# A decoder layer on one core: the first batch's weights, chunks and scales in another order

## The chip, the core and the metric

The kernel runs on one core of a Trainium2 chip. Five engines work side by side, each in the order of its own instructions: TensorE (PE, matmuls and transposes; its weight loads are listed apart as PEld), VectorE (DVE), ScalarE (ACT), GpSimd (POOL) and SyncE (SP), which here only issues DMAs. They wait for each other through semaphores. The metric is the device time of one execution in microseconds (us), the median of several runs.

## The reference, cut to what matters

The layer has three parts, each with a layer norm ahead and a residual behind: self attention, cross attention and a feed-forward block. x is 8 batches of 256 rows of 1024. The change touches the start of the self attention alone:

```python
def bitnet_linear(x, weight, scale_param):
    s = jnp.maximum(jnp.mean(jnp.abs(weight), axis=1), 1e-08)
    binary_w = jnp.sign(weight / s[:, None])
    y = jnp.einsum('bsi,oi->bso', x, binary_w)
    y = y * (s * scale_param)[None, None, :]
    return jnp.nan_to_num(y, nan=0.0, posinf=1000000.0, neginf=-1000000.0)
...
q, k, v = three bitnet_linear of layernorm(x)    # 32 heads for q, 8 for k and v, 32 wide
scores = jnp.einsum('bhqd,bhkd->bhqk', q, k) / np.sqrt(HEAD_DIM)
attn = jax.nn.softmax(scores, axis=-1)
out = jnp.einsum('bhqk,bhkd->bhqd', attn, v)
return bitnet_linear(out, o_weight, o_scale)
```

So every weight row gives a scale (the mean of its absolute values) and a row of signs. q, k and v need signs to multiply with, and scales to multiply the product with.

## The kernel before, in words

**Weights.** The four weight matrices are cut into 20 blocks of 128 rows by 1024: two of k, eight of q, two of v, eight of o. `blocks` lists them in the order in which they are loaded; the place in this list is the block's number. Before, 0 and 1 are k, 2 and 3 are q's first two, 4 and 5 are v, 6 to 11 the rest of q, 12 to 19 o. For a block, `weight_load` (lines 276 to 296) issues its DMAs on SP: one of 512 KB for k and v, four of 128 KB for q, eight of 64 KB for o. `weight_turn` turns it by 8 PE transposes into two PSUM banks, and ACT writes the signs from there (Sign, L313). `weight_sum` takes the sum of absolute values on DVE (L302), then a small operation on DVE (s, L304) and three on POOL (L305 to L307), which leave the scale in `scol`. Eight blocks have room at once; the list `after` says which block is loaded into the room of which, when that has been turned and summed. SP issues in order, so a load that waits for its room holds up those behind it.

**Projections.** x of a batch, normed and turned, is kept as a high and a low part (`xh`, `xl`), so that a chunk of 128 columns of q or k takes 16 matmuls. In the first batch, `first_chunk` (L425 the matmuls, L431 to L440 what follows) makes a chunk alone: ACT scales it (y), and five operations of DVE, six for k, make it finite and scale it. Later chunks come in pairs as parts (`q_parts`, L403, L412): there `nan_to_num` spreads the work over DVE and POOL, and its last operation, a copy_predicated on DVE (L361), is put off until two parts later (`later`, `settle`). v scales columns, not rows, so that its scales, and o's, have to lie along the free dimension: `scale_part` makes diagonal tiles of `scol` on POOL (dg, L331) ahead of time, multiplies them with ones on PE (L338), and DVE copies the result to `v_sc` or `o_sc` (L339).

**Order.** Everything is issued in an order that is written out by hand. A prologue loads, norms x of batch 0, turns blocks 0 to 3 and makes both k chunks and two q chunks. Then `step` runs 8 times for each batch, once for every four heads (c, from 0 to 7); below, step c is that of the first batch. A step issues the scores of its four heads (L549), DVE's row maxima (nm, L692), the turning of the previous step's probabilities (L528, copied by ACT, L532), then the parts that `self_plan` lists for this step, with the exponentials of ACT (L711) and the divisions by the sums (`over_sums`: on DVE, POOL or ACT, as the table `BY` says with a letter for each head) between them, and last the product with v (L587). Steps 0 to 3 use k chunk 0, steps 4 to 7 k chunk 1.

The parts of the first batch's steps before:

```python
[weight(4), weight(5), v0[0], weight(6), weight(7)]
+ [scale_part(10, 2, v_sc), v0[1]],
mixed(q_parts(st, 2) + q_parts(st, 4), [weight(8), weight(9), weight(10)]),
[weight(11)] + q_parts(st, 6) + [weight(12)],
[weight(13)] + ln[:2] + [weight(14)] + ln[2:],
k[:1] + [weight(15)] + k[1:],
...
```

Here `weight(i)` is turn, sum and the next load, `ln` are the four parts that norm and turn x of batch 1 (xn, L155; the turns at L163; xh, L348; xl, L349), and `k`, `v` are projections of batch 1.

**PSUM.** All these parts take their PSUM tiles from `bank`, in a fixed turn over three banks; a tile waits until the one three places before it (or two of three, by the pool) has been read. The scores have four banks of their own.

Of the kernel before, what the change touches and what calls it, by code (L numbers as in the profile page):

```python
# [13 lines left out]
AF = mybir.ActivationFunctionType  # L14
# [21 lines left out]
def decoder_layer(  # L36
# [214 lines left out]
    def block(put, t, col, w, q=False, o=False):  # L251
        a = State()
        a.put, a.t, a.col, a.rows, a.q, a.o = put, t, col, w, q, o
        blocks.append(a)

    def columns(dst, t):
        return lambda e0: dst[:, e0 : e0 + 4, t * P : (t + 1) * P]

    for t in range(2):
        block(columns(kT_w, t), t, 8 + t, kw)  # L260
    for c in range(2):
        block(columns(qT_w[c], 0), c, c, qw, q=True)
    for t in range(2):
        block(columns(vT_w, t), t, 10 + t, vw)
    for c in range(2, EC):
        block(columns(qT_w[c], 0), c, c, qw, q=True)
    for t in range(EC):
        block(columns(oT_w, t), t, 12 + t, ow, o=True)

# [9 lines left out]
    def weight_load(i):  # L279
        a = blocks[i]  # L280
        a.w = wk_.tile([P, E], F32, tag=where[i], name="w")
        if a.q:
            gh, r = a.t // 4, a.t % 4
            for j in range(4):
                r0 = ((gh * 4 + j) * 4 + r) * HD
                nc.sync.dma_start(a.w[j * HD : (j + 1) * HD, :], a.rows[r0 : r0 + HD, :])
        elif a.o:

            rows = a.rows[a.t * P : (a.t + 1) * P, :]
            for c in range(EC):  # L290
                nc.sync.dma_start(
                    a.w[:, c * P : (c + 1) * P].rearrange("p (j d) -> p j d", d=HD),
                    rows.rearrange("p (g j r d) -> p g r j d", g=2, j=4, r=4)[:, c // 4, c % 4],
                )
        else:
            nc.sync.dma_start(a.w, a.rows[a.t * P : (a.t + 1) * P, :])

    def weight_sum(i):

        a = blocks[i]  # L300
        total = small.tile([P, 1], F32, tag="rs", name="total")
        nc.vector.tensor_reduce(total, a.w, AX.X, ALU.add, apply_absolute_value=True)  # L302
        s = small.tile([P, 1], F32, tag="s", name="s")
        nc.vector.tensor_scalar(s, total, 1.0 / E, 1e-8, ALU.mult, ALU.max)  # L304
        nc.gpsimd.tensor_scalar_mul(total, total, 0.0)  # L305
        nc.gpsimd.tensor_add(s, s, total)
        nc.gpsimd.tensor_mul(scol[:, a.col : a.col + 1], s, pcol[:, a.col : a.col + 1])  # L307

    def weight_turn(i):

        a = blocks[i]
        for h in range(2):
            nc.scalar.activation(  # L313
                a.put(4 * h), four_T(a.w[:, h * 512 : (h + 1) * 512], "ps_w"), AF.Sign
            )

    def weight_next(i):

        weight_turn(i)
        weight_sum(i)  # L320
        for k in after.get(i, []):
            weight_load(k)

    def scale_part(col0, n, dst, soon=False):

        box = {}

        def ahead():
            box["dg"] = wk_.tile([P, n, P], F32, tag="xn", name="dg", bufs=2)
            for k in range(n):  # L330
                nc.gpsimd.tensor_scalar_mul(  # L331
                    box["dg"][:, k, :], ident, scol[:, col0 + k : col0 + k + 1]
                )

        def main():
            ps = bank([P, n, P], "ps_d")
            for k in range(n):
                nc.tensor.matmul(ps[:, k, :], ones, box["dg"][:, k, :], start=True, stop=True)  # L338
            nc.vector.tensor_copy(dst, ps.rearrange("p k c -> p (k c)"))  # L339

        return Part(0.3 * n, main, ahead, soon)

    def weight(i):
        return Part(1.1, lambda: weight_next(i))


    def split(hi, lo, src):
# [19 lines left out]
    def ln_parts(st, b):  # L367


        def ahead(q):  # L370
            t, h = q // 2, q % 2
            need(st)
            st.xn = getattr(st, "xn", {})
            st.xn[q] = normed_half(xb[b][t], st.mv[:, t, 0:1], st.rs[:, t : t + 1], h)

        def main(q):
            t, h = q // 2, q % 2
            if q == 0:
                st.xh = wk_.tile([P, EC, S], F32R, tag="xh", name="xh")
                st.xl = wk_.tile([P, EC, S], F32R, tag="xl", name="xl")  # L380
            ps = four_T(st.xn.pop(q), "ps_t")
            e4, t4 = slice(h * 4, (h + 1) * 4), slice(t * P, (t + 1) * P)
            split(st.xh[:, e4, t4], st.xl[:, e4, t4], ps)

        return [Part(0.5, lambda q=q: main(q), lambda q=q: ahead(q), True) for q in range(2 * TB)]
# [56 lines left out]
    def q_parts(st, c0):  # L442
        return proj_T(
            st, lambda i, e: qT_w[c0 + i][:, e, :], c0, lambda: st.qT[:, c0 : c0 + 2, :]
        )
# [3 lines left out]
    def k_parts(st):  # L449
        def dst():  # L450
            st.kT = wk_.tile([P, 2, S], F32, tag="kT", name="kT", bufs=2)
            st.qT = wk_.tile([P, EC, S], F32, tag="qT", name="qT", bufs=2)
            return st.kT

        def then():
            nc.vector.tensor_scalar_mul(st.kT, st.kT, K_SCALE)

        return proj_T(st, lambda i, e: kT_w[:, e, i * P : (i + 1) * P], 8, dst, then)
# [645 lines left out]
    def tail(fb, j):  # L1104
# [14 lines left out]


    BY = {
        0: ["DDDD", "PPPD", "PPPD", "PPPP", "PPPD", "PPPD", "DDDD", "PPPD"],
        1: ["DDAA", "PPAA", "PPAA", "DDDA", "DDAA", "DDDA", "DDDA", "DDDA"],
        B - 1: ["DDAA", "DDDA", "DDAA", "PPAA", "PPAA", "DDDA", "DDDA", "DDDA"],
    }
# [8 lines left out]
    def mixed(a, b):  # L1134
        out = []
        for i in range(max(len(a), len(b))):
            out += a[i : i + 1] + b[i : i + 1]
        return out
# [4 lines left out]
    def self_plan(b):  # L1143
        st = sts[b]
        if b == 0:
            nxt = sts[1]
            v0 = v_parts(st)
            ln, k, v = ln_parts(nxt, 1), k_parts(nxt), v_parts(nxt)
            return [
                [weight(4), weight(5), v0[0], weight(6), weight(7)]  # L1150
                + [scale_part(10, 2, v_sc), v0[1]],
                mixed(q_parts(st, 2) + q_parts(st, 4), [weight(8), weight(9), weight(10)]),
                [weight(11)] + q_parts(st, 6) + [weight(12)],
                [weight(13)] + ln[:2] + [weight(14)] + ln[2:],
                k[:1] + [weight(15)] + k[1:],
                mixed(v, [weight(16), weight(17)]),
                mixed(q_parts(nxt, 0), [weight(18), scale_part(12, 4, o_sc[:, 0:512], True)])
                + [weight(19)],
                mixed(q_parts(nxt, 2), [scale_part(16, 4, o_sc[:, 512:1024])]),
            ]  # L1160
        o = o_all(sts[b - 1])
        if b + 1 < B:
            nxt = sts[b + 1]
            ln = ln_parts(nxt, b + 1)
            return [
                q_parts(st, 4) + q_parts(st, 6),
                o[0][:1] + ln[:2] + o[0][1:],
                o[1][:1] + ln[2:] + o[1][1:],
                k_parts(nxt),
                o[2] + v_parts(nxt),  # L1170
                o[3],
                q_parts(nxt, 0),
                q_parts(nxt, 2),
            ]
        x0 = xts[0]
        ln = lnx_parts(x0)
        return [
            q_parts(st, 4) + q_parts(st, 6),
            o[0],
            o[1],  # L1180
            o[2][:1] + ln[:2] + o[2][1:],
            o[3][:1] + ln[2:] + o[3][1:],
            ctx_parts(x0, (act, dve)) + ckv_part(x0),
            cq_part(x0) + ckvT_part(x0),
            cqk_parts(x0, (dve, act)),
        ]
# [62 lines left out]
    with tc.manual_schedule(  # L1249
# [12 lines left out]
        ln_moments(st, 0)  # L1262
        need(st)
        weight_turn(0)
        st.xh = wk_.tile([P, EC, S], F32R, tag="xh", name="xh")
        st.xl = wk_.tile([P, EC, S], F32R, tag="xl", name="xl")
        lo = []
# [13 lines left out]
        for a in lo:  # L1281
            nc.vector.tensor_sub(*a)
        weight_turn(1)
        for i in range(2):
            weight_sum(i)
        for i in range(2):
            for k in after.get(i, []):
                weight_load(k)
        st.kT = wk_.tile([P, 2, S], F32, tag="kT", name="kT", bufs=2)
        st.qT = wk_.tile([P, EC, S], F32, tag="qT", name="qT", bufs=2)  # L1290
        for i in range(2):
            first_chunk(
                st, lambda e: kT_w[:, e, i * P : (i + 1) * P], 8 + i, st.kT[:, i, :], K_SCALE
            )
            weight_next(2 + i)
        for i in range(2):
            first_chunk(st, lambda e: qT_w[i][:, e, :], i, st.qT[:, i, :])
        xb[1] = load_x(1)

        prev = None  # L1300
# [94 lines left out]
```

## Time and profile before

| | |
|---|---|
| time, median of 3 runs | 1546.89 us (1545.93 to 1547.07) |
| the profiled execution, its own time | 1546.57 us |
| its span in the profile | 1544.8 us |
| PE busy | 1511.1 us, 98% of the span |
| DVE, ACT, POOL busy | 62%, 52%, 26% |
| mean granted clock of TensorE | 0.995 |
| PE busy, 0 to 70 us and 70 to 130 us | 54.2 and 52.7 us |
| PE busy, 130 to 1545 us | 1404.2 us |

A line of the timeline gives start and length in us, engine, line of the kernel, operation, output and inputs, shape and number of instructions, and in brackets how long the engine sat idle before it and what ended that. A row of the table of stretches gives the stretch and its length, the busy time and number of instructions of PE, PEld, DVE, ACT and POOL, the clock granted to TensorE (1.00 is full speed), the share of the DMA engines and what they moved.

### The profile page before, as it was taken

To read this page: it belongs to the slowest core of one execution; us is meant where nothing else is said; L and a number is where in the kernel's file an instruction comes from. 1 tells how busy PE (TensorE), PEld (TensorE's weight loads), DVE (VectorE), ACT (ScalarE), POOL (GpSimd) and SP (SyncE) were. 2 spreads that over 40 slices of the span, in tenths; PEclk is the share of its full clock that TensorE was granted. 3 is DMA by queue.
4 is the path that set the end of the run, shared out by engine and by line. 5 is a ranking of instruction groups with operands and counts; after the bars stand their busy time and mean duration, and the time that the engine had idled before them with its cause. 6 is when DMAs were issued, how large, how long until landed. Compare 5 with 4: busy or idle time off the path is not lost.

```text
span 1544.8 us, 25713 instructions
## 1 busy us (share of the span) xinstructions
PE 1511.1 (98%) x9494; PEld 1015.2 (66%) x9494; DVE 956.7 (62%) x1878; ACT 799.2 (52%) x2450; POOL 402.8 (26%) x475
## 2 busy tenths in 40 slices
PE   6899999999999999999999999999999999999998
PEld 5777888888888887777777777544444444444443
DVE  7878898999989899766676665343233233323322
ACT  4677898989898888755566666311111111111110
POOL 2555453545354534022221211131001100100000
PEclk9989999999999999999999999999999999999999
DMA  9430020101020141212444311110011002000001
GB/s 234 68 83 18 26 69 29 56 29 65 19 69 28 60 153 45 85 42 71 152 152 168 107 63 77 62 41 0 0 56 54 0 7 102 1 0 27 28 0 54
DMA packets 67917, 92.78 MB, mean 60 GB/s; under 512 B 40475, under 2 KB 46417, under 8 KB 67665
## 3 DMA queue, kind: packets, MB, share of 16 engines
q1 hardware_dynamic: 63184, 74.37, 15.6%
q0 software_dynamic: 4608, 16.78, 2.7%
q8 instruction: 75, 1.23, 0.3%
q14 instruction: 50, 0.40, 0.1%
HBM read 65.44 MB, written 25.17 MB: 59 GB/s over the span
## 4 chain that ended last, share of the span: by engine, by line
PE 88%; DVE 5%; ACT 3%; DMA 2%; POOL 1%; issue 1%; SPq 0%; DVEq 0%; ACTq 0%; POOLq 0%
PE ps_h L1045 19%; PE ps_pt L528 10%; PE ps_z L1089 9%; PE ps_q L403 8%; PE ps_o L496 7%; PE s L549 4%; PE po L587 4%; PE ps_p L1019 4%; PE ps_o L1108 4%; PE s L625 3%; PE po L648 3%; PE ps_q L855 2%; PE ps_qk L870 2%; PE ps_t L163 2%; PE ps_o L665 2%; PE ps_v L470 2%
## 5 line engine op out<-in xcount | busy, mean ns | idle before, releaser
L711 ACT ACTIVATE p<-s,nm 128x256 f32<-128x256 f32 x768 | 359.7, 520 | 0.4 <-DVE nm L692 0.4
L532 ACT COPY pT<-ps_pt 128x512 f32<-128x512 f32 x384 | 197.3, 599 | 170.1 <-PE ps_pt L528 169.6
L1057 ACT ACTIVATE sg<-ps_h,b_col 128x512 f32<-128x512 f32 (+1 forms) x88 | 59.6, 678 | 413.5 <-PE ps_h L1045 413.5
L692 DVE TENSOR_REDUCE nm<-s 128x2 f32<-128x512 f32 x384 | 237.5, 678 | 9.2 <-PE s L625 6.0
L1058 DVE SCALAR_TENSOR_TENSOR sg<-ps_h,b_col,sg 128x512 f32<-128x512 f32 (+1 forms) x88 | 65.0, 739 | 273.1 <-ACT sg L1057 273.1
L528 PE MATMUL ps_pt<-ident,p 128*128 128x128 f32 x1536 | 194.6, 279 | 1.8 <-DVE o_sc L339 1.0
L711 ACT ACTIVATION_READ_ACCUMULATOR p<-s,nm 128x1 f32 x768 | 193.4, 252 | 0.0
L528 PEld LDWEIGHTS ps_pt<-ident,p 128*128 128x128 f32 x1536 | 164.3, 141 | 41.5 <-issue 26.6
L1089 PE MATMUL ps_z<-ac,u_sb 128*128 128x512 f32 x336 | 157.7, 593 | 0.0
L403 PE MATMUL ps_q<-xh,qT_w 128*128 128x256 f32 x496 | 121.7, 287 | 0.0
L403 PE MATMUL ps_q<-xl,qT_w 128*128 128x256 f32 x496 | 118.9, 281 | 0.0
L1345 POOL TENSOR_TENSOR x2t<-x2t,b_sb 128x1024 f32<-128x1024 f32 x16 | 37.6, 2357 | 296.2 <-DVE xn L155 296.2
L680 POOL TENSOR_TENSOR x1t<-x1t,y 128x256 f32<-128x256 f32 x64 | 47.3, 759 | 232.7 <-DVE y L673 230.2
L1089 PEld LDWEIGHTS ps_z<-ac,u_sb 128*128 128x128 f32 x336 | 61.9, 190 | 68.8 <-issue 68.8
L356 POOL TENSOR_SCALAR tmp<-y 128x512 f32<-128x512 f32 x78 | 58.4, 749 | 182.1 <-DVE y L505 103.1
L496 PE MATMUL ps_o<-oT_w,oh 128*128 128x512 f32 x256 | 105.9, 414 | 0.0
L496 PE MATMUL ps_o<-oT_w,ol 128*128 128x512 f32 x256 | 101.0, 395 | 0.0
L403 PEld LDWEIGHTS ps_q<-xh,qT_w 128*128 128x128 f32 x496 | 93.3, 188 | 1.6
L403 PEld LDWEIGHTS ps_q<-xl,qT_w 128*128 128x128 f32 x496 | 93.4, 188 | 0.0
L572 DVE TENSOR_SCALAR p<-p,sm 128x256 f32<-128x256 f32 x250 | 87.4, 406 | 7.9
L1045 PE MATMUL ps_h<-pT,w_ffn 128*128 128x512 f32 (+1 forms) x184 | 88.7, 577 | 0.0
L1045 PE MATMUL ps_h<-late,w_ffn 128*128 128x512 f32 (+1 forms) x184 | 88.7, 577 | 0.0
(159 smaller groups left out, 2731.7 us busy)
## 6 DMA issues: line engine op xcount, KB each, us to landing
xs<-in_x_dram SPq DMA_DIRECT2D x32, 512.0 KB, 4.2
x<-xs POOLq DMA_DIRECT2D x16, 512.0 KB, 3.0
x1t<-x SPq DMA_DIRECT2D x16, 512.0 KB, 6.0
c<-in_ctx_dram SPq DMA_DIRECT2D x16, 512.0 KB, 3.9
x<-x1t POOLq DMA_DIRECT2D x16, 512.0 KB, 3.8
x2t<-x SPq DMA_DIRECT2D x16, 512.0 KB, 5.0
out_dram<-x2t SPq DMA_DIRECT2D x32, 256.0 KB, 2.0
w<-in_L_attn_q_weight_dram SPq DMA_DIRECT2D x32, 128.0 KB, 5.8
```

Source lines behind the costliest of these rows:

```text
L403: nc.tensor.matmul(ps[:, i, :], w(i, e), x_[:, e, :], start=(e == 0 and x_ is st.xh), stop=(e == EC - 1 and x_ is st.xl),)
L496: nc.tensor.matmul(ps, o_[c // 4][:, c % 4, t * P : (t + 1) * P], oT_w[:, c, h * 512 : (h + 1) * 512], start=(c == 0 and o_ is st.oh), sto ...
L528: nc.tensor.transpose(ps[:, k, t * P : (t + 1) * P], p[:, t, k * P : (k + 1) * P], ident)
L532: nc.scalar.copy(pT, ps)
L549: nc.tensor.matmul(s[j][:, t, :], st.qT[p0 : p0 + 32, c, t * P : (t + 1) * P], st.kT[p0 : p0 + 32, c // 4, :], start=True, stop=True,)
L572: nc.vector.tensor_scalar_mul(p, p, self.sm[:, t, j : j + 1])
L587: nc.tensor.matmul(self.po[p0 : p0 + 32, :], self.st.v[:, k, g * HD : (g + 1) * HD], pTs[j][:, k, :], start=(k == 0), stop=(k == TB - 1),)
L692: nc.vector.tensor_reduce(nm[:, j, :], s[j], AX.X, ALU.max, negate=True)
L711: nc.scalar.activation(cur.p[j][:, t, :], s[j][:, t, :], AF.Exp, bias=nm[:, j, t : t + 1], accum_out=cur.sm[:, t, j : j + 1],)
L1045: nc.tensor.matmul(ps[h * n : h * n + n], v1_of(r, i, f, n), fb.pT[:, r, h * w_ : (h + 1) * w_], start=(r == 0), stop=(r == RC - 1),)
L1058: nc.vector.scalar_tensor_tensor(sg[:m], hs[0][:m], bg, sg[:m], ALU.add, ALU.mult)
L1089: nc.tensor.matmul(fb.zs[r], fw.u2[f // 4][:n, f % 4, r * P : (r + 1) * P], ac[:n], start=(k == 0), stop=(k == NF - 1 and COPIES < 2),)
```

## The change

The order of the first batch is written anew. The block list becomes k's first, q's first two, v's two, two more of q, k's second, the rest of q, o. The prologue makes k chunk 0 and q chunk 0 alone, then turns blocks 2, 3 and 4 (q's second, v's two); the sums of v's two blocks are taken by ACT (Abs with an accumulator, written in place), with the small operation s on POOL. sum(0) and the load behind it are issued ahead of the norming of x. q chunk 1 is the first part of step 0, followed by the turns of blocks 5 and 6, the scales of v, the two sums, and then both parts of v. k chunk 1 is made in step 1, behind q chunks 2 and 3. The later turns, q parts and x parts are spread anew over steps 2 to 7; the scales of o's second half move to the first step of batch 1. `scale_part` copies on ACT instead of DVE. In step 3 two heads are divided by ACT instead of POOL, in step 7 three by DVE instead of POOL.

```diff
-    for t in range(2):
-        block(columns(kT_w, t), t, 8 + t, kw)
-    for c in range(2):
-        block(columns(qT_w[c], 0), c, c, qw, q=True)
+    ON_ACT = (3, 4)
+    K, V, Q = [0, 7], [3, 4], [1, 2, 5, 6, 8, 9, 10, 11]
+    block(columns(kT_w, 0), 0, 8, kw)
+    q_blocks(0, 1)
     for t in range(2):
         block(columns(vT_w, t), t, 10 + t, vw)
-    for c in range(2, EC):
-        block(columns(qT_w[c], 0), c, c, qw, q=True)
+    q_blocks(2, 3)
+    block(columns(kT_w, 1), 1, 9, kw)
+    q_blocks(4, 5, 6, 7)
...
-    def weight_sum(i):
+    def weight_sum(i, on_act=False):
...
-        nc.vector.tensor_reduce(total, a.w, AX.X, ALU.add, apply_absolute_value=True)
+        if on_act:
+
+            nc.scalar.activation(a.w, a.w, AF.Abs, accum_out=total)
+            eng = nc.gpsimd
+        else:
+            nc.vector.tensor_reduce(total, a.w, AX.X, ALU.add, apply_absolute_value=True)
+            eng = nc.vector
         s = small.tile([P, 1], F32, tag="s", name="s")
-        nc.vector.tensor_scalar(s, total, 1.0 / E, 1e-8, ALU.mult, ALU.max)
+        eng.tensor_scalar(s, total, 1.0 / E, 1e-8, ALU.mult, ALU.max)
...
-            nc.vector.tensor_copy(dst, ps.rearrange("p k c -> p (k c)"))
+            nc.scalar.copy(dst, ps.rearrange("p k c -> p (k c)"))
...
-        0: ["DDDD", "PPPD", "PPPD", "PPPP", "PPPD", "PPPD", "DDDD", "PPPD"],
+        0: ["DDDD", "PPPD", "PPPD", "PPAA", "PPPD", "PPPD", "DDDD", "DDDD"],
...
             return [
-                [weight(4), weight(5), v0[0], weight(6), weight(7)]
-                + [scale_part(10, 2, v_sc), v0[1]],
-                mixed(q_parts(st, 2) + q_parts(st, 4), [weight(8), weight(9), weight(10)]),
-                [weight(11)] + q_parts(st, 6) + [weight(12)],
-                [weight(13)] + ln[:2] + [weight(14)] + ln[2:],
-                k[:1] + [weight(15)] + k[1:],
-                mixed(v, [weight(16), weight(17)]),
-                mixed(q_parts(nxt, 0), [weight(18), scale_part(12, 4, o_sc[:, 0:512], True)])
-                + [weight(19)],
-                mixed(q_parts(nxt, 2), [scale_part(16, 4, o_sc[:, 512:1024])]),
+                [Part(2.0, lambda: q_chunk(1))]
+                + [Part(0.9, lambda i=i: turn(i)) for i in Q[2:4]]
+                + [scale_part(10, 2, v_sc), Part(0.0, sums)] + v0,
+                [weight(8), weight(7)] + q_parts(st, 2)
+                + [Part(2.0, lambda: k_chunk(1)), weight(9)],
+                [weight(10)] + mixed(q_parts(st, 4), [weight(11)]),
+                q_parts(st, 6) + ln[:2] + [weight(12)],
+                ln[2:] + [weight(13)] + k[:1] + [weight(14)] + k[1:],
+                mixed(v, [weight(15), weight(16)]),
+                mixed(q_parts(nxt, 0), [weight(17), scale_part(12, 4, o_sc[:, 0:512], True)])
+                + [weight(18)],
+                mixed(q_parts(nxt, 2), [weight(19)]),
             ]
...
+            scales = [scale_part(16, 4, o_sc[:, 512:1024])] if b == 1 else []
             return [
-                q_parts(st, 4) + q_parts(st, 6),
+                q_parts(st, 4) + scales + q_parts(st, 6),
...
         weight_turn(0)
+        weight_sum(0)
+        weight_free(0)
...
         weight_turn(1)
-        for i in range(2):
-            weight_sum(i)
-        for i in range(2):
-            for k in after.get(i, []):
-                weight_load(k)
+        weight_sum(1)
+        weight_free(1)
...
-        for i in range(2):
-            first_chunk(
-                st, lambda e: kT_w[:, e, i * P : (i + 1) * P], 8 + i, st.kT[:, i, :], K_SCALE
-            )
-            weight_next(2 + i)
-        for i in range(2):
-            first_chunk(st, lambda e: qT_w[i][:, e, :], i, st.qT[:, i, :])
+        k_chunk(0)
+        q_chunk(0)
+        for i in (2, 3, 4):
+            weight_turn(i)
+        weight_sum(2)
+        for i in V:
+            weight_sum(i, True)
+        for i in (2, 3, 4):
+            weight_free(i)
         xb[1] = load_x(1)
```

`weight_free(i)` issues the loads into block i's room; `q_chunk` and `k_chunk` are calls of `first_chunk`, and `sums` is the sum and the load behind it for blocks 5 and 6.

More of the change, by code (lines that the diff above doesn't have):

```diff
@@ L257, in columns, with q_blocks @@
         return lambda e0: dst[:, e0 : e0 + 4, t * P : (t + 1) * P]
-    for t in range(2):
-        block(columns(kT_w, t), t, 8 + t, kw)
-    for c in range(2):
-        block(columns(qT_w[c], 0), c, c, qw, q=True)
+    def q_blocks(*chunks):
+        for c in chunks:
+            block(columns(qT_w[c], 0), c, c, qw, q=True)
+    ON_ACT = (3, 4)
+    K, V, Q = [0, 7], [3, 4], [1, 2, 5, 6, 8, 9, 10, 11]
+    block(columns(kT_w, 0), 0, 8, kw)
+    q_blocks(0, 1)
     for t in range(2):
         block(columns(vT_w, t), t, 10 + t, vw)
-    for c in range(2, EC):
-        block(columns(qT_w[c], 0), c, c, qw, q=True)
+    q_blocks(2, 3)
+    block(columns(kT_w, 1), 1, 9, kw)
+    q_blocks(4, 5, 6, 7)
     for t in range(EC):
@@ L315, in weight_turn, with weight_free, weight_next @@
             )
-    def weight_next(i):
-        weight_turn(i)
-        weight_sum(i)
+    def weight_free(i):
         for k in after.get(i, []):
             weight_load(k)
+    def weight_next(i, on_act=False):
+        weight_turn(i)
+        weight_sum(i, on_act)
+        weight_free(i)
     def scale_part(col0, n, dst, soon=False):
@@ L338, in main @@
                 nc.tensor.matmul(ps[:, k, :], ones, box["dg"][:, k, :], start=True, stop=True)
-            nc.vector.tensor_copy(dst, ps.rearrange("p k c -> p (k c)"))
+            nc.scalar.copy(dst, ps.rearrange("p k c -> p (k c)"))
         return Part(0.3 * n, main, ahead, soon)
     def weight(i):
-        return Part(1.1, lambda: weight_next(i))
+        return Part(1.1, lambda: weight_next(i, i in ON_ACT))
     def split(hi, lo, src):
@@ L1148, in self_plan, with turn, sums @@
             ln, k, v = ln_parts(nxt, 1), k_parts(nxt), v_parts(nxt)
-            return [
-                [weight(4), weight(5), v0[0], weight(6), weight(7)]
-                + [scale_part(10, 2, v_sc), v0[1]],
-                mixed(q_parts(st, 2) + q_parts(st, 4), [weight(8), weight(9), weight(10)]),
-                [weight(11)] + q_parts(st, 6) + [weight(12)],
-                [weight(13)] + ln[:2] + [weight(14)] + ln[2:],
-                k[:1] + [weight(15)] + k[1:],
-                mixed(v, [weight(16), weight(17)]),
-                mixed(q_parts(nxt, 0), [weight(18), scale_part(12, 4, o_sc[:, 0:512], True)])
-                + [weight(19)],
-                mixed(q_parts(nxt, 2), [scale_part(16, 4, o_sc[:, 512:1024])]),
+            def turn(i):
+                weight_turn(i)
+            def sums():
+                for i in Q[2:4]:
+                    weight_sum(i)
+                    weight_free(i)
+            return [
+                [Part(2.0, lambda: q_chunk(1))]
[10 more added lines that the diff above has]
+                mixed(q_parts(nxt, 2), [weight(19)]),
             ]
@@ L1283, in decoder_layer, with k_chunk @@
         weight_turn(1)
-        for i in range(2):
-            weight_sum(i)
-        for i in range(2):
-            for k in after.get(i, []):
-                weight_load(k)
+        weight_sum(1)
+        weight_free(1)
         st.kT = wk_.tile([P, 2, S], F32, tag="kT", name="kT", bufs=2)
         st.qT = wk_.tile([P, EC, S], F32, tag="qT", name="qT", bufs=2)
-        for i in range(2):
+        def k_chunk(i):
             first_chunk(
@@ L1294, in decoder_layer, with q_chunk @@
             )
-            weight_next(2 + i)
-        for i in range(2):
+        def q_chunk(i):
             first_chunk(st, lambda e: qT_w[i][:, e, :], i, st.qT[:, i, :])
+        k_chunk(0)
+        q_chunk(0)
+        for i in (2, 3, 4):
+            weight_turn(i)
+        weight_sum(2)
+        for i in V:
+            weight_sum(i, True)
+        for i in (2, 3, 4):
+            weight_free(i)
         xb[1] = load_x(1)
```

## The prediction

> **What bounds the kernel now.** I read the page first (sections 1 and 2), then TensorE's waits up to 140 us, a table of stretches, and the timelines of PE, DVE, ACT, POOL and SP up to 130 us.
>
> ```profile
> PE 1511.1 (98%) x9494; PEld 1015.2 (66%) x9494; DVE 956.7 (62%) x1878; ACT 799.2 (52%) x2450; POOL 402.8 (26%) x475
> ```
>
> TensorE bounds the whole. The stretches show that what it loses lies early:
>
> ```profile
> 37.90:41.30 3.40, 3.22 (x16) 2.97 (x16) 1.47 (x5) 0.00 (x0) 0.98 (x4) 0.50 0.74 115
> 75.45:85.70 10.25, 7.97 (x50) 4.43 (x49) 6.51 (x12) 5.29 (x16) 5.66 (x10) 0.50 0.38 58
> 130.00:1545.00 1415.00, 1404.20 (x8577) 924.64 (x8576) 852.56 (x1667) 718.57 (x2220) 342.72 (x356) 1.00 0.16 55
> ```
>
> (length, PE, PEld, DVE, ACT and POOL busy, granted clock, DMA share, GB/s.) After 130 us PE is idle for 10.8 of 1415 us. So a microsecond saved in the first batch reaches the end undiminished, and a new wait there costs in full. Two stretches ran at half clock, 3.2 + 8.0 us of PE work. PE's idle gaps, in brackets with what ended them:
>
> ```profile
> 26.28 1.15 PE L549 MATMUL s<-kT,qT 32*128 32x256 f32 x16 [0.94 <-DVE qT L438]
> 37.60 0.54 PE L338 MATMUL ps_d<-dg,ones 128*128 128x128 f32 x2 [3.06 <-POOL dg L331]
> 51.22 1.09 PE L163 MATMUL ps_w<-ident,w 128*128 128x128 f32 x8 [1.43 <-ACT y L412]
> 74.07 0.63 PE L163 MATMUL ps_t<-ident,xn 128*128 128x128 f32 x4 [2.25 <-DVE xn L155]
> 77.30 1.11 PE L163 MATMUL ps_w<-ident,w 128*128 128x128 f32 x4 [1.07 <-DVE xl L349]
> 118.35 1.53 PE L528 MATMUL ps_pt<-ident,p 128*128 128x128 f32 x12 [1.03 <-DVE o_sc L339]
> ```
>
> **What is lost before**, between 8.73 us (first weight landed, unchanged) and 130 us. Idle gaps of the PE timeline: 0.23, 0.43, 0.94, 0.32, 0.74, 3.06, 0.18, 1.43, then step 3's 2.25 + 0.16 + 1.07 + 0.53 + 0.68, then 0.73, 0.52, 1.03: together 14.3. Half clock: half of the 3.2 and 8.0 us of work, 5.6. The second scale matmuls (L338, 8 in 2.25 us against 1.05 for the same eight at 112 us, paced by POOL's dg): 1.2. Sum 21.1 us.
>
> **The change, step by step.** PE does the same work in both, so I lay the new order out with the rows' durations and count the gaps. Unit prices: 16 chunk matmuls 1.9 us, a weight turn 1.0, scores 1.08, four p turns 1.97, a Sign of 128x512 0.49, an exp with its accumulator read 0.46, a DVE weight sum with its s 1.35, the four row maxima (nm) 2.48.
>
> *Start.* sum(0) on DVE now stands ahead of the four xn: mv ends 9.18, sum and s to 10.6, so xn starts at 10.6 instead of 10.33. PE loses 0.23 + 0.27 = 0.5.
>
> *Prologue.* k chunk 0 ends at 17.3, q chunk 0 at 19.2. The turns of blocks 2, 3, 4 follow, paced by PSUM banks that ACT's Signs free: to 22.3. qT of chunk 0: y at 19.9, DVE 1.55 more, 21.5, ahead of PE. Scores start at 22.3, not 26.28; the 0.43, 0.94, 0.32 and 0.74 go.
>
> *Two sums by ACT.* No row has Abs or 1024 columns. ACT's 256 columns cost 0.37 (L604), 512 cost 0.59 (L1279), so 1024 about 1.03, with the 0.23 read at most 1.26; low end 0.85, if reads hide. I take 1.13 each: 22.9 to 25.2. ACT's y of q chunk 1 is queued behind, but its matmuls end at 25.3. So they cost PE nothing; without that cover each 0.1 over is 0.1 on the Signs behind. Should Abs need function tables of its own, two loads of 1.28 (the row at 0.72 us; so far Sign, Exp and Copy share that one load) would stand on ACT ahead of the Signs of step 0: 2.6 at most, kept as an upper end.
>
> *Step 0.* q chunk 1 to 25.2, turns 5 and 6 to 27.25. POOL has both v scales by 26.5 (four small operations of about 0.3 each) and dg by 27.85 (two of 0.67). ps_d ends near 28.1: PE loses 0.85 instead of 3.06 + 0.18 and keeps its clock (1.6). v runs 28.4 to 32.2, scores(1) and p turns to 35.4. Before was there at 45.0 with 2.9 us more work done.
>
> *Step 1.* exps wait for nm behind v's DVE work (first nm 35.95). A turn of block 7 waits for a bank, 0.5. Then q 2 and 3 to 41.75, k chunk 1 to 43.65, turn, po to 45.65. Scores(2) needs qT of chunk 2, whose last operation (copy_predicated, L377 new) now stands on DVE behind the six of k chunk 1. Reckoned from the last exp (ACT, 41.65): reciprocal 0.2, two p of 0.29 to 0.93 each (0.93 where POOL multiplies too), statistics 0.6, qT and fin 0.8, statistics 0.7, then these rows and 0.65:
>
> ```profile
> 21.58 0.28 DVE L434 TENSOR_SCALAR kT<-y 128x256 f32<-128x256 f32 x1
> ...
> 22.23 0.41 DVE L437 TENSOR_TENSOR kT<-kT,tmp 128x256 f32<-128x256 f32 x1
> 22.67 0.45 DVE L438 COPY_PREDICATED kT<-fin,y 128x256 f32<-128x256 uint8 x1
> 23.16 0.30 DVE L440 TENSOR_SCALAR kT<-kT 128x256 f32<-128x256 f32 x1
> ```
>
> 1.8 in all. It ends between 47.1 and 48.4. New wait: 1.5 to 2.7; I take 2.35, since POOL has p at that time. This is the change's main price. Row before: a 2.25 us gap in 72.0 to 75.4 was followed by half clock, a 1.43 one was not. So I add one 3.4 us window at half clock, 1.6. The Trainium skill ("TensorE: Matmul & The Clock Gate", What you observe / What's actually happening) puts the throttle after an idle window of about 3.4 us; by that rule no half clock follows, and the sum would be 1.6 less. The trace disagrees: 3.06 idle sufficed.
>
> *Steps 2 to 4.* Step 2 has two turns and two chunks: no gap. Step 3 now carries q 6 and 7, two transposes of the next batch's x and one turn, so the two q parts (3.8 us) cover nm and xn, where before the x parts came at once and waited 2.25. Left are 1.05 (turn behind xl, bank) and, in step 4, 1.3 (the fourth xn behind sum(12) and nm, both on DVE). Neither fills a window. Step 3's last two heads go from POOL to ACT, 4 x 0.37, after q's y and before nothing that PE needs.
>
> *Steps 5 to 7.* 0.73 and 0.52 stay. Scales of o's second half leave for batch 1, behind a long finished dg: 1.03 and 1.2 go. Heads of step 7 go from POOL to DVE: 6 x 0.29 = 1.7 more, beside 8.9 us of PE work; a DVE full in that step would give up to 1 us back.
>
> *DMA.* SP's order puts block 4's successor, 8 DMAs of o (5.3 us of issue), ahead of x of batch 1. It lands near 39, and DVE takes it at 43.3: no cost. POOL's added s operations: 0.3 each, in the dg term.
>
> Left after: 0.5 + 0.85 + 0.5 + 2.35 + 1.6 + 1.05 + 1.3 + 1.25 = 9.4. I add 1.0 for hand-overs that such a layout misses (rows before show five gaps of 0.16 to 0.43). 21.1 - 10.4 = 10.7 us gained. The profiled execution took 1546.57 (span 1544.8 and 1.8 around it); 1535.9, and with the median 0.3 above it, 1536.2.
>
> **Rivals.** (1) The wait at scores(2) is at its upper end and half clock lasts the three windows it lasted before (78% busy at half clock did not raise it, 78.9 to 82.3): 0.35 + 2.4 more, and steps 3 and 4 double their 2.35 on a later DVE: gain 5.6, 1541.3. For: the same kind of gap did this. Against: step 2 has chunks to keep PE full. 0.18. (2) No half clock follows the wait, because it stays small enough or a window's edge parts it: 1.6 less, 1534.6, with smaller hand-overs 1533. For: the 1.43 gap passed. Against: 2.25 and 3.06 did not. 0.20. This is the case that the Trainium skill's clock-gate rule above would give.
> (3) Slower: x of batch 1 lands late behind o's small packets. DVE's statistics then block qT in order, and each us after 43.3 is one on PE. It decides from 54 (gain gone); landing at 60 gives 1536.2 + 16.7 = 1553. Against: x took 4.0 us from issue, the margin is over 4. 0.06. (4) No change: the gaps only move, DVE (busy 25.0 of the 28.3 us from 8.73 to 37) being the true bound: 1546.9. Against: two sums and a v_sc copy leave DVE, and PE's work is the same. 0.06.
>
> **How the numbers follow.** Forecast 0.50. With (1) and (2) the faster cases hold 0.88; 0.2% is 3.1 us, about what a measurement of this kernel can tell from no change. Range: from 1532, below (2), to 1542, above (1); it leaves out (3), (4) and some tails.
>
> **What would show it.** Scores(0) near 22.3; ps_d's gap under 1 us and full clock at 38; scores(2) preceded by a 1.5 to 2.7 us gap ended by DVE qT, then one short half-clock stretch; step 3's xn gap gone; PE after the first batch as dense as now, some 11 us earlier. Wrong if PE waits for x, if Abs brings table loads, or if half clock outlasts step 2.

## The result, and the profile after

The changed kernel takes 1537.17 us (median of 4 runs, 1536.99 to 1537.37) against 1546.93 for the one before (4 runs, 1545.93 to 1547.07): a ratio of 0.9939, 95% interval 0.9927 to 0.9951. The spans of the profiled executions are 1544.8 and 1535.6 us. Of all runs below, one, in experiment 5, took 2168.36 us at a granted clock of 0.656, and that experiment's median and ratio leave it out.

First the busy times of the whole span, from the profile's page:

```profile
PE 1505.1 (98%) x9494; PEld 1012.4 (66%) x9494; DVE 952.9 (62%) x1877; ACT 801.9 (52%) x2461; POOL 398.7 (26%) x472
```

PE is busy 6.0 us less with as many matmuls: the two stretches at half clock, which cost 5.6 us before, are gone. The clock is full from 12.26 us on to the end of the first batch and beyond. The stretches show it, and that the rest of the kernel has not changed:

```profile
12.26:46.39 34.13, 31.90 (x280) 28.37 (x279) 30.23 (x70) 25.69 (x70) 14.13 (x35) 1.00 0.93 213
46.39:49.80 3.41, 2.03 (x25) 1.67 (x26) 3.34 (x7) 0.20 (x1) 0.11 (x1) 1.00 0.14 22
70.00:130.00 60.00, 55.00 (x531) 47.12 (x528) 51.02 (x108) 45.04 (x138) 28.90 (x52) 1.00 0.17 36
120.00:1535.00 1415.00, 1404.68 (x8579) 925.80 (x8577) 852.72 (x1668) 717.35 (x2219) 346.08 (x360) 1.00 0.16 55
```

From 120 us on PE is busy for 1404.68 of 1415 us; before, it was 1404.20 of 1415 from 130 on. What the first batch saves reaches the end almost whole. The first scores of batch 1 (the ninth of all) start at 114.36 instead of 126.82 us, 12.5 us earlier; the tenth at 128.60 instead of 138.56, 10.0 earlier, since o's second scales and a wait of 0.93 now stand between these two. Another 0.8 is lost behind: from the tenth scores to the end it is 1406.2 us before and 1407.0 after. That is not the scales' doing, as experiment 9 has them in the same place and takes 1406.3; in the profiles of this document this stretch takes 1406.2 to 1407.1 us, and what moves it is open.

PE's timeline, with the waits that answer to those shown of before:

```profile
21.48 1.15 PE L565 MATMUL s<-kT,qT 32*128 32x256 f32 x16
26.56 1.09 PE L354 MATMUL ps_d<-dg,ones 128*128 128x128 f32 x4
37.06 0.66 PE L163 MATMUL ps_w<-ident,w 128*128 128x128 f32 x4 [0.74 <-ACT qT_w L325]
47.77 1.15 PE L565 MATMUL s<-kT,qT 32*128 32x256 f32 x16 [2.40 <-DVE qT L377]
68.15 0.66 PE L163 MATMUL ps_w<-ident,w 128*128 128x128 f32 x4 [1.62 <-DVE xl L365]
75.43 0.63 PE L163 MATMUL ps_t<-ident,xn 128*128 128x128 f32 x4 [2.14 <-DVE xn L155]
102.07 1.13 PE L354 MATMUL ps_d<-dg,ones 128*128 128x128 f32 x8 [1.16 <-ACT oT_w L325]
115.99 1.13 PE L565 MATMUL s<-kT,qT 32*128 32x256 f32 x10 [0.93 <-ACT p L727]
```

The 3.06 us wait for POOL's dg has shrunk to two short gaps of 0.12 and 0.14; scores(0) start 4.8 us earlier, and from there to scores(9) PE waits 10.4 us in all. The largest wait is the one at scores(2), for DVE's copy_predicated of q chunk 2.

### The profile page after: what moved, and what is told of

It is laid out like the page before. It is cut to its first block, busy times and chain, and to the rows that moved or that the text cites. A ratio compares the mean times of both kernels' runs of the same rounds, so it can differ in the third digit from the quotient of the medians.

```text
span 1535.6 us, 25707 instructions
## 1 busy us (share of the span) xinstructions
PE 1505.1 (98%) x9494; PEld 1012.4 (66%) x9494; DVE 952.9 (62%) x1877; ACT 801.9 (52%) x2461; POOL 398.7 (26%) x472
## 4 chain that ended last, share of the span: by engine, by line
PE 89%; DVE 6%; ACT 3%; issue 1%; DMA 1%; SPq 0%; POOL 0%; DVEq 0%; ACTq 0%; POOLq 0%
PE ps_h L1061 19%; PE ps_pt L544 10%; PE ps_z L1105 9%; PE ps_q L419 8%; PE ps_o L512 7%; PE s L565 4%; PE ps_p L1035 4%; PE ps_o L1124 4%; PE po L603 4%; PE s L641 4%; PE po L664 3%; PE ps_q L871 2%; PE ps_qk L886 2%; PE ps_v L486 2%; ACT p L727 2%; PE ps_o L681 2%
```

## The experiments

They ask four things: what the wait at scores(2) is worth, whether the gaps of steps 3 and 4 can be moved or only passed on, which parts of the change carry the gain, and what ends the wait of step 7. Scores(c) are those of step c; 8 and 9 belong to batch 1. Each median stands beside the kernel before's in the same series. Steps of an experiment's profile are compared with the changed kernel's first profile, or, where it is said, with its second, of experiment 3, which like some of the others has a window at half clock behind scores(2).

**1. The wait at scores(2): q parts ahead of the turns of step 1.**

```diff
-                [weight(8), weight(7)] + q_parts(st, 2)
+                q_parts(st, 2) + [weight(8), weight(7)]
                 + [Part(2.0, lambda: k_chunk(1)), weight(9)],
```

> The changed kernel, with q chunks 2 and 3 as the first parts of step 1, ahead of the turns of blocks 8 and 7 and of k chunk 1. Theory (the 2.40 us wait at scores(2) is only the place of qT's copy_predicated on DVE, behind k chunk 1): the wait falls under 0.4 and the kernel is 2.0 to 2.4 us faster than the changed one, near 1535.0. Rival (DVE is full in this stretch, so what is saved at scores(2) is waited for in steps 2 and 3): under 0.7 us faster, with a new wait of about 2 us on DVE before 70 us.

Measured 1537.78 us against 1546.7 (0.9944, 0.9929 to 0.9959). Scores(1) to scores(2) take 13.69 us instead of 15.99: the wait is gone. Scores(2) to scores(3) take 11.84 instead of 9.80: 2.04 of the 2.30 is given back. DVE's timeline of this kernel shows by whom:

```profile
43.95 0.73 DVE L377 COPY_PREDICATED qT<-fin,y 128x512 f32<-128x512 uint8 x1
49.49 0.29 DVE L456 TENSOR_SCALAR kT<-kT 128x256 f32<-128x256 f32 x1
51.61 2.48 DVE L708 TENSOR_REDUCE nm<-s 128x2 f32<-128x512 f32 x4
```

qT is ready 1.4 us ahead of the scores at 46.07, but DVE has the rest of step 1 to do first, and takes the maxima of these scores only at 51.61, 5.5 us after they started; in the changed kernel it does so 1.75 us after. From 43.95 to 54.00 DVE is busy for 9.34 of 10.05 us, so in this order it is the bound. Its one wait there, 0.53, is for k chunk 1's y, which ACT could not start before:

```profile
47.43 0.47 ACT L447 ACTIVATE y<-ps_q,scol 128x256 f32<-128x256 f32 x1 [4.90 <-POOL scol L319]
```

This scale is of block 7, whose sum stands on DVE behind block 8's; the two the other way round were not tried. In step 3 this execution lost 2.4 us more, with a window at half clock from 69.48. The rival held: the kernel is no faster than the changed one.

**2. The same wait made longer.** DVE does the copy_predicated of k chunk 1 three times.

```diff
         nc.vector.copy_predicated(dst, fin, y)
+        if col == 9:
+            nc.vector.copy_predicated(dst, fin, y)
+            nc.vector.copy_predicated(dst, fin, y)
```

> The changed kernel, with the copy_predicated of k chunk 1 done three times instead of once (the same values; two more of 0.49 us on DVE ahead of qT). The wait at scores(2) grows from 2.4 to 3.4 us. Theory (the clock falls to half once about 2 us of a 3.41 us window are idle): a half-clock stretch of 3.4 us follows, and the kernel is 2.2 to 2.8 us slower than the changed one. Rival (only a window that is idle as a whole lowers the clock): 0.8 to 1.1 us slower, granted clock 1.00 throughout.

Measured 1540.27 us (0.9964, 0.9951 to 0.9976). The wait is 3.32 instead of 2.40, and scores(1) to (2) are longer by 0.99: the two copies of 0.49 on DVE reach scores(2) one for one. The stretch behind it ran at half clock (49.48 to 52.89), so that scores(2) to (3) took 11.20 instead of 9.80. Step 4 gave 0.67 back (its wait for xn 1.46 instead of 2.14), as it did behind the half-clock window of experiment 3. From scores(0) to scores(9) this is 1.9 us more, a little under the 2.2 to 2.8 expected.

**3. The changed kernel again.**

> The changed kernel once more, beside the two below. Its start differs between executions by when the first weight lands (8.6 to 10.1 us so far) and by where the clock's windows of 3.413 us fall. Theory: the wait of 2.4 us at scores(2) brings half clock when a window holds over about 2 us of it, as it did at one place with the same wait, and not when a window's edge parts it: 1536.5 to 1540, the profile's steps 0 to 8 as long as before to 0.3 us where no half clock falls in. Rival: 1537.2 to 0.3 in each execution.

Measured 1539.21 us (1537.39 to 1540.97, against 1546.24; 0.9953, 0.9939 to 0.9966). Here are the stretches around its wait at scores(2), again 2.40 us:

```profile
46.36:49.78 3.42, 1.17 (x18) 0.42 (x16) 3.32 (x11) 1.22 (x3) 1.18 (x1) 1.00 0.42 66
49.78:53.19 3.41, 3.27 (x22) 2.47 (x23) 3.09 (x6) 0.04 (x1) 0.59 (x3) 0.50 0.02 5
```

Scores(2) to (3) took 11.28 instead of 9.80: the same wait cost 1.48 us more. The first profiled execution shows why it was spared: the grid of 3.41 us windows lay so that the wait was parted at 46.39, and the window behind still had PE busy for 2.03 us. Here the first weight landed 1.6 us later, and 2.3 of the 2.4 us fell into one window. Of the changed kernel's nine runs in both series, the six with a mean granted clock of 1.000 took 1537.0 to 1538.4 us, the three with 0.999 took 1539.2 to 1541.0.

**4. The turn ahead of the q parts in step 3, one more between the x parts in step 4.**

```diff
-                q_parts(st, 6) + ln[:2] + [weight(12)],
-                ln[2:] + [weight(13)] + k[:1] + [weight(14)] + k[1:],
+                [weight(12)] + q_parts(st, 6) + ln[:2],
+                ln[2:3] + [weight(13)] + ln[3:] + k[:1] + [weight(14)] + k[1:],
```

> The changed kernel, with block 12's part ahead of q chunks 6 and 7 in step 3 and block 13's part between the last two x parts in step 4. Theory (step 3's 0.38 + 1.62 us are PSUM banks that x's low half on DVE holds, and step 4's 2.14 us is the fourth xn behind sum(12) and nm): the bank waits go, and the fourth xn comes 1.3 us earlier and is covered by a turn: 1.5 to 2.5 us faster than the changed kernel. Rival (DVE's work up to nm(4) sets the pace): the 2.0 us reappear in front of the fourth x part, under 0.6 us faster.

Measured 1538.92 us (0.9951, 0.9936 to 0.9966). Scores(3) to (5) took 26.41 us instead of 25.76. PE's timeline:

```profile
70.00 0.63 PE L544 MATMUL ps_pt<-ident,p 128*128 128x128 f32 x4 [0.78 <-DVE xl L365]
73.01 1.07 PE L544 MATMUL ps_pt<-ident,p 128*128 128x128 f32 x8 [2.38 <-DVE xl L365]
76.69 0.66 PE L163 MATMUL ps_t<-ident,xn 128*128 128x128 f32 x4 [1.24 <-DVE xl L365]
```

The turn was the cover: without it, x's PSUM banks wait for DVE's xl and hold up the p turns. The waits of both steps come to 4.95 us, against 4.67 in the changed kernel: moved, not saved.

**5. Both of these.** The edits of 1 and 4 together.

> The changed kernel with both reorderings at once (q chunks 2 and 3 first in step 1; block 12's part first in step 3, block 13's between x parts in step 4). If each does what its theory says and they lie in different steps, the gains add: 3.5 to 4.5 us faster than the changed kernel, near 1533. Rival (DVE is behind by the end of step 2 and steps 3 and 4 give back what step 1 gained): no faster than the better of the two alone.

Measured 1539.64 us (median of 4; 0.9953, 0.994 to 0.9967): no better than either alone. The profiles say so without the series between them: scores(1) to (5) take 52.47 us, with the edits alone 52.63 and 52.21, in the changed kernel 51.55. The rival held.

**6. x all in step 3, as before the change, q parts in step 2.**

```diff
-                [weight(10)] + mixed(q_parts(st, 4), [weight(11)]),
-                q_parts(st, 6) + ln[:2] + [weight(12)],
-                ln[2:] + [weight(13)] + k[:1] + [weight(14)] + k[1:],
+                [weight(10)] + mixed(q_parts(st, 4), [weight(11)]) + q_parts(st, 6),
+                ln[:2] + [weight(12)] + ln[2:],
+                [weight(13)] + k[:1] + [weight(14)] + k[1:],
```

> The changed kernel, with steps 2 to 4 nearer to the order before: q chunks 6 and 7 go back into step 2, and all four x parts of batch 1 come in step 3 around block 12's turn, with no q part beside them. Theory (the two q parts in step 3 are what covers nm and xn): waits of 4 to 6 us for xn and xl in step 3 come back, 2 to 4 us slower than the changed kernel, and 4 us more where the clock falls to half. Rival (the gain of step 3 came from DVE and POOL being less far behind, not from the q parts): within 1 us of the changed kernel.

Measured 1541.29 us (0.9969, 0.9957 to 0.9981). Scores(2) to (5) took 38.27 us instead of 35.56. PE's waits and the stretch behind them:

```profile
67.80 0.63 PE L163 MATMUL ps_t<-ident,xn 128*128 128x128 f32 x4 [2.12 <-DVE xn L155]
70.76 0.63 PE L163 MATMUL ps_t<-ident,xn 128*128 128x128 f32 x4 [1.46 <-DVE xn L155]
72.94 0.71 PE L163 MATMUL ps_t<-ident,xn 128*128 128x128 f32 x4 [1.56 <-DVE xn L155]
```

```profile
73.36:76.77 3.41, 3.41 (x30) 1.77 (x32) 0.90 (x3) 2.84 (x9) 0.04 (x1) 0.50 0.02 5
```

With 0.63 ahead of them the waits come to 5.8 us, against 4.7 in the changed kernel's steps 3 and 4 (0.38, 1.62, 2.14, 0.53). Spreading x over two steps saves 1.1 of waiting and the half-clock stretch, 1.7. So the q parts do cover nm and xn, but for less than the sum had taken, which let 4.7 us of gaps shrink to 2.35.

**7. V's two sums on DVE.**

```diff
-    ON_ACT = (3, 4)
+    ON_ACT = ()
...
-            weight_sum(i, True)
+            weight_sum(i)
```

> The changed kernel, with the two sums of v's blocks on DVE again (two times 1.35 us ahead of nm(0)). Theory (DVE carries step 0: nm, q chunk 1, two sums, eight p): 2 to 2.7 us slower than the changed kernel, seen at the p turns of step 1, and ps_d waits for POOL no longer than 1 us. Rival (DVE's idle of about 0.7 us between 22 and 26 us and the exps' pace take most of it): under 1 us slower.

Measured 1540.56 us (0.996, 0.9945 to 0.9975). Scores(0) to (3) took 38.09 us instead of 36.09; PE's timeline has one wait that is new and one that is longer:

```profile
36.66 1.09 PE L544 MATMUL ps_pt<-ident,p 128*128 128x128 f32 x8 [1.35 <-DVE y L495]
51.13 1.15 PE L565 MATMUL s<-kT,qT 32*128 32x256 f32 x16 [2.80 <-DVE qT L377]
```

The two sums (2.7 of DVE by the row of before) cost 2.0 on the path. What they cost ACT is seen in its timeline of the changed kernel:

```profile
22.14 1.11 ACT L310 ACTIVATE w<-w 128x1024 f32<-128x1024 f32 x1
23.09 0.24 ACT L310 ACTIVATION_READ_ACCUMULATOR w<-w 128x1 f32 x1
```

0.95 from start to read, and no load of a table ahead of it.

**8. The heads divided as before.**

```diff
-        0: ["DDDD", "PPPD", "PPPD", "PPAA", "PPPD", "PPPD", "DDDD", "DDDD"],
+        0: ["DDDD", "PPPD", "PPPD", "PPPP", "PPPD", "PPPD", "DDDD", "PPPD"],
```

> The changed kernel, with the table of heads of the kernel before (step 3: PPPP instead of PPAA, step 7: PPPD instead of DDDD). Theory (POOL's two p of 1.04 in step 3 stand ahead of its share of qT, and so of qT's copy_predicated and x's low half on DVE, which already waited 1.26 us there): 1 to 2 us slower than the changed kernel, in steps 3 and 4. Rival (the tables change nothing that PE waits for): within 0.4 us.

Measured 1540.41 us (0.9962, 0.9948 to 0.9975). Scores(3) to (5) took 28.29 us instead of 25.76: the waits for xl and xn are 2.14 and 3.11 instead of 1.62 and 2.14, and the second emptied a window:

```profile
76.56:79.97 3.41, 0.30 (x4) 0.32 (x4) 3.41 (x8) 1.81 (x6) 0.59 (x3) 1.00 0.00 0
79.97:83.38 3.41, 3.41 (x19) 3.32 (x17) 2.28 (x4) 2.84 (x10) 0.98 (x1) 0.50 0.00 0
```

After its wait at scores(2) this execution also had a half-clock stretch, as in 3, so that profile is the nearer one: there scores(3) to (5) took 25.19 us and the waits of both steps 4.1, here 5.6. Against it the two letters of step 3 carry 1.5 us of waits and, by the half clock behind, 1.7 of time. The prediction had them at nothing. Step 7's letters, moved back in the same edit, show no effect: scores(7) to (9) took 23.40 us in both, with the same wait of 0.93.

**9. The kernel before, with o's second scales in batch 1 alone.** Of the whole change only the move of `scale_part(16, 4, ...)`.

```diff
-                mixed(q_parts(nxt, 2), [scale_part(16, 4, o_sc[:, 512:1024])]),
+                q_parts(nxt, 2),
...
+            scales = [scale_part(16, 4, o_sc[:, 512:1024])] if b == 1 else []
             return [
-                q_parts(st, 4) + q_parts(st, 6),
+                q_parts(st, 4) + scales + q_parts(st, 6),
```

> The kernel before, with one part of the change alone: the scales of o's second half leave step 7 for the first step of batch 1 (still copied by DVE). Theory (its 1.03 us wait and the 1.2 us by which POOL's diagonal tiles pace the matmuls go, and nothing comes in their place): 1.9 to 2.3 us faster than the kernel before. Rival (PE then meets scores(8) or the p turns as early as ACT and DVE let it): under 1 us faster.

Measured 1545.46 us against 1546.38 (0.9993, 0.9984 to 1.0002). Scores(7) to (8) took 9.13 us instead of 11.23, and scores(8) to (9) 12.68 instead of 11.74, where the part now is: 1.2 saved, the term for its pacing by POOL. The medians, 0.9 apart with a ratio of 1 inside the interval, can't show it by themselves. The 1.01 wait ahead of the p turns stayed; so it was not this half's.

**10. The same, and the copy behind the scales on ACT.**

```diff
-            nc.vector.tensor_copy(dst, ps.rearrange("p k c -> p (k c)"))
+            nc.scalar.copy(dst, ps.rearrange("p k c -> p (k c)"))
```

> The kernel before, with the scales of o's second half in the first step of batch 1 (as in the run of that alone) and scale_part's copy on ACT instead of DVE. Theory (the 1.03 us wait of the p turns in step 7 is for the copy of the first half's scales, queued on DVE; moving the second half's left it at 1.01): this wait goes, 0.8 to 1.1 us faster than with the late scales alone, 1.9 to 2.3 than the kernel before. Rival (ACT, with its exps, is as late as DVE): no faster than the late scales alone.

Measured 1545.08 us against 1546.24 (0.9996, 0.9987 to 1.0005): nothing more than 9 that can be told. The 1.01 wait, for the copy of the first half, is gone, but PE's timeline at scores(8) shows what came instead:

```profile
122.09 1.07 PE L587 MATMUL po<-pT,v 128*32 128x256 f32 x16 [0.41 <-DVE ol L608]
123.09 1.78 PE L549 MATMUL s<-kT,qT 32*128 32x256 f32 x16
```

These scores took 1.15 in 9. A wait of 0.41 and matmuls that were fed late, 0.63, are the 1.01 again. ACT's exps ahead of them had waited 1.40 us for DVE's nm.

**11. Three more sums on ACT.** Where the changed kernel still waits from 60 to 120 us, DVE is on the path at every gap but the 0.38 at 65.88, busy 51.0 of the 60 us from 70 to 130; ACT has 45.0.

```diff
-    ON_ACT = (3, 4)
+    ON_ACT = (3, 4, 12, 16, 18)
```

> The changed kernel, with the sums of blocks 12, 16 and 18 by ACT as well, which is idle for 1.2 to 2.1 us just behind each of the three turns, while DVE has the sum ahead of nm(4), nm(6) and nm(7). Theory (these sums on DVE set the fourth xn and the exps of steps 6 and 7): the wait for xn falls from 2.14 to about 0.9, the 1.16 at ps_d and the 0.93 at scores(8) to under 0.4: 2.5 to 3.5 us faster than the changed kernel run beside it. Rival (as with the two reorderings, DVE or ACT gives it back a step later): under 1 us.

Measured 1536.18 us (1534.75 to 1536.57; 0.9933, 0.992 to 0.9945): 3.0 below the changed kernel in the same series (1537.39 to 1540.97), with no overlap. Both profiles have the half-clock window behind scores(2). PE's timeline where the changed kernel waits 1.74, 1.44 and 0.53 in that series (1.62, 2.14 and 0.53 in its first profile):

```profile
71.76 0.66 PE L163 MATMUL ps_w<-ident,w 128*128 128x128 f32 x4 [1.72 <-DVE xl L365]
77.60 0.63 PE L163 MATMUL ps_t<-ident,xn 128*128 128x128 f32 x4 [0.69 <-DVE xn L155]
79.83 0.39 PE L419 MATMUL ps_q<-xh,kT_w 128*128 128x256 f32 x1 [0.73 <-DVE xl L365]
```

The wait for xn falls by 0.75, half of what the 2.14 of the first profile would say, and scores(4) to (5) by 0.55. The larger part comes later: scores(6) to (9) take 32.73 us instead of 35.61, 2.9 less, for the waits at ps_d, po and scores(8) (1.16, 0.25, 0.93) are gone, with no gap above 0.15 from 80 us to the end of the first batch. They hung on DVE's sums.

**12. And two heads of step 3 from POOL to DVE.**

```diff
-        0: ["DDDD", "PPPD", "PPPD", "PPAA", "PPPD", "PPPD", "DDDD", "DDDD"],
+        0: ["DDDD", "PPPD", "PPPD", "DDAA", "PPPD", "PPPD", "DDDD", "DDDD"],
```

> As the one with three more sums by ACT, and step 3's first two heads by DVE instead of POOL (DDAA). Theory (POOL's p stand ahead of its share of qT and slow DVE's fin to 1.26 us there): qT's copy_predicated comes 1.4 us earlier, x's low half 0.7: another 0.7 to 1.4 us faster. Rival (the four p on DVE, 1.14 us, cost what POOL's absence saves): within 0.4 us of the one without.

Measured 1535.35 us (1534.62 to 1536.59; 0.9929, 0.9917 to 0.9942). The gain was expected from an idle time of DVE in step 3, as its timeline in the changed kernel's first profile has it, while POOL, behind its p, had not finished qT:

```profile
66.24 1.26 DVE L374 TENSOR_SCALAR fin<-y 128x512 uint8<-128x512 f32 x1
69.36 0.74 DVE L377 COPY_PREDICATED qT<-fin,y 128x512 f32<-128x512 uint8 x1 [1.26 <-POOL qT L373]
```

But in that kernel's second profile, and in 11, this wait is 0.56 already. What 12 changes is seen against DVE's timeline of 11:

```profile
68.63 0.18 DVE L578 RECIPROCAL sm<-sm 128x4 f32<-128x4 f32 x1 [0.75 <-ACT p L727]
69.36 0.99 DVE L371 TENSOR_SCALAR qT<-y 128x512 f32<-128x512 f32 x1 [0.55 <-ACT y L428]
72.27 0.76 DVE L377 COPY_PREDICATED qT<-fin,y 128x512 f32<-128x512 uint8 x1 [0.56 <-POOL qT L373]
```

and in this one:

```profile
67.77 1.14 DVE L588 TENSOR_SCALAR p<-p,sm 128x256 f32<-128x256 f32 x4
69.11 0.43 DVE L371 TENSOR_SCALAR qT<-y 128x512 f32<-128x512 f32 x1
71.45 0.75 DVE L377 COPY_PREDICATED qT<-fin,y 128x512 f32<-128x512 uint8 x1 [0.56 <-POOL qT L373]
```

The p of the two heads fill idle time in which DVE waited for ACT, and the first operation of qT takes 0.43 instead of 0.99, with POOL no longer dividing beside it. The wait for POOL stays 0.56. Counted from scores(3) (61.08 in 11, 60.83 here), the copy_predicated starts 0.57 earlier, the wait for xl is 1.15 instead of 1.72, and scores(3) to (4) take 11.70 instead of 12.27. So more work for DVE made it faster. By the medians it is 0.8 better than 11, but the ranges overlap; the profile's 0.57 is the better evidence. It has the lowest median of all kernels here, 3.9 below the changed kernel in its series.

## Why the prediction was right, and where it was not

The forecast was 1536.2 us and the result 1537.17, faster, inside the range. The sum held: 10.4 us were to be left of 21.1, and 11.1 are (10.6 of gaps, 0.5 of a later first weight). The 10.0 between are what scores(9) came earlier. Its terms held less well, and that their errors nearly cancel is luck: half clock, the hand-overs and v's scales were 3.2 too high together, the other terms 3.9 too low. In the second series, where three of five runs had a mean clock below 1.000, the median was 1539.21, 3.0 above the forecast and still inside the range.

- **First batch earlier: right.** Scores(0) at 21.48 (predicted 22.3), though the first weight landed 0.5 us later; the clock was full at 12.26 instead of 14.01 us, which the sum did not hold.
- **Two sums by ACT: right.** 22.14 to 24.37 measured, 22.9 to 25.2 predicted, hidden behind the matmuls of q chunk 1, no tables. Experiment 7 puts their worth at 2.0 us.
- **The scales of v: gap over.** ps_d waits 0.26 instead of the 0.85 taken.
- **The wait at scores(2): right**, 2.40 against 2.35, with DVE as its cause. Experiment 1 adds what the prediction had not said: the other order tried in step 1 removes it, but behind it DVE is nearly full, and the time is lost there.
- **Half clock, 1.6: mis-sized in the first execution, right in the next.** 0 there, 1.48 in experiment 3. The prediction gave this a case of its own (the second rival, a window's edge that parts the wait). Its hand-overs were not the smaller ones which that rival took, so its 1533 was not reached.
- **Steps 3 and 4: too low.** 2.00 and 2.67 measured for 1.05 and 1.3. Together that is 4.67, as much as the 4.69 of gaps in step 3 before: what went there is the half clock (4.0), not the waiting. The layout counted sum(12) and nm as what delays xn and xl, and left out that fin of a q part takes 1.26 us while POOL divides p (0.42 to 0.43 at 60 and 83 us, where it does not), and that DVE then idles for POOL, 1.26 in this profile and 0.56 in the next. Experiments 11 and 12 take 0.75 and 0.57 off these waits.
- **Step 3's heads: the worth missed.** They stood in the sum at nothing; experiment 8 has steps 3 and 4 longer without ACT, by 2.5 us against the first profile and 3.1 against the second.
- **Steps 5 to 7: too low, on a wrong cause.** The 1.03 was laid to o's second half and so was to go with it. Experiments 9 and 10 show that it hung on the copy of the first half, and that DVE's load behind it is the true bound: without the copy it came back at scores(8). In the changed kernel 1.16, 0.25 and 0.93 stand there, 2.34 for the 1.25 taken. A DVE full in step 7, which was to give up to 1 us back, is what happened, but not by the heads that the prediction named: with these on POOL again (experiment 8) the 0.93 stays, and only experiment 11, which takes sums from DVE, removed it. The 1.2 of dg's pacing was right (1.2).
- **x of batch 1: in time**, as taken; DVE's statistics start at 42.05. The third rival did not occur. The fourth, that DVE bounds and the gaps only move, is right of single waits (experiments 1, 4, 5, 10) and wrong of the whole, since the change takes work from DVE.

Of the parts of the change, experiments price four: 2.0 us for the sums on ACT, 2.5 to 3.1 for the heads of step 3 and 2.7 for the spread of x, clock included in both, and 1.2 for the late scales (this one in the kernel before). The new order of prologue, v and k chunk 1, behind which POOL's wait of 3.06 us and its half clock went, was read from the two traces only; it was not undone by itself, so its share of the 9.8 us is not shown. These shares do not add, since the waits feed one another.

## What to carry to other kernels

When one engine's gaps all end on another, moving parts about only moves the gap: look for work that can leave that other engine, as the sums here did, or for idle time of its own, as 12 found. A wait is priced by its length and by the busy share of the clock window in which it falls, so a range for it needs both ends. Of a stall ended by a copy, ask what would end it next before its whole length is counted as a gain.

## What the runs showed of the hardware

The granted clock changes at the edges of windows 3.41 us long: in the kernel before at 14.01, 37.90, 41.30, 75.45 and 85.70 us, which lie 7, 1, 10 and 3 windows apart. Their phase differs from execution to execution; in the changed kernel the first such edge is at 12.26. In all fourteen profiles, the windows at full clock with PE busy for up to 1.31 us (experiment 9) were followed by one at half clock, and those with 1.50 us or more kept it full; between these none was seen. At half clock more was needed: windows with 1.90 and 2.66 us of work (75.45 and 78.86 in the kernel before) were followed by another at half, one with 3.22 (37.90) was not. The lower border shows in the kernel before and the changed kernel:

```profile
72.04:75.45 3.41, 1.23 (x10) 1.05 (x11) 3.41 (x8) 2.90 (x10) 0.00 (x0) 1.00 0.00 0
```

```profile
73.70:77.11 3.41, 1.50 (x12) 1.28 (x12) 2.91 (x6) 2.28 (x9) 0.00 (x0) 1.00 0.00 0
```

The first was followed by half clock, the second not. The Trainium skill ("TensorE: Matmul & The Clock Gate", What you observe / What's actually happening) tells of a free-running window, and the traces agree, by the edges above; it asks for an idle window, and here windows with up to 1.31 us of work in them lowered the clock.

The first weight landed between 8.6 and 10.9 us after the start, in kernels that issue its load in the same way; nothing in the traces says why. The changed kernel's times spread from 1537.0 to 1541.0 us over both series. Its two profiles differ by the landing of this weight and by the window's phase; that these two make up the whole spread is not shown.
